# A gated two-layer block on one core: row statistics, the last head's sum and a few queue places are changed around the end of the long convolution and the start of attention

## The chip, the cores and the metric

The kernel runs on one core of a Trainium2 chip, which has eight. A core has five engines, each with its own in-order queue: TensorE (PE) for matrix products and transposes, VectorE (DVE), ScalarE (ACT), GpSimd (POOL), and SyncE (SP), which here only starts transfers. They work beside each other and wait for each other through semaphores. Sixteen DMA engines move data. The metric is the device time of one execution in microseconds (us), as a median of several. The profile is of one further execution.

## The reference, cut to what matters

The input `x` has 8 sequences of 256 rows of 512 numbers, 2048 rows in all, that is 16 tiles of 128 rows. Four parts add to it one after the other:

```python
x = x + tanh(g_xattn[0]) * L0_xattn(ctx, ctx, layernorm(x), ssm_kernel, D, 8)  # long convolution
x = x + tanh(g_ffn[0])   * L0_ffn(layernorm(x), w1, w2, w3)   # 512 -> 1408 -> 512
x = x + tanh(g_xattn[1]) * L1_xattn(layernorm(x), ctx, mask)  # attention over 256 keys
x = x + tanh(g_ffn[1])   * L1_ffn(layernorm(x), w1, w2, w3)   # 512 -> 2048 -> 512
```

The first part takes 32 heads of 8 channels. For each head it forms the products of all pairs of channels of `ctx`, convolves each pair along the 512 positions with the head's kernel (causal, with a skip term `D`), multiplies by the normalised `x` of the head, and sums over one of the two channel indices:

```python
kv  = einsum('bhil,bhjl->bijhl', k_, v_)      # k = v = ctx: symmetric in i, j
out = causal_conv(kv, ssm_kernel) + kv * D
out = einsum('bijhl,bhil->bjhl', out, q_)     # q = layernorm(x)
```

In the first feed-forward part each row is rounded to 8 bits by its own largest value, and the weights to -1, 0 or 1 by the mean of their absolute values:

```python
xq = clip(round(x * s), -128, 127) / s        # s = 127 / max|x| of the row
wq = clip(round(w * scale), -1, 1) / scale    # scale = 1 / mean|w|
h  = silu(xq @ w1q.T) * (xq @ w2q.T)
out = quantised(h) @ w3q.T
```

The second feed-forward part uses `sign(w)` times the mean absolute weight, and rounds its input in groups of 64.

## The kernel before, in words

The order of every engine's work is the order of the program text: the kernel asks for a manual schedule, so an instruction waits behind all that was written before it for the same engine.

**The convolution** runs over the heads, one head a step (`h`, steps 0 to 31). In the trace of before a step takes about 5 us: step 12 begins near 86, step 21 near 134, step 24 near 150, step 28 near 171 and step 31 near 187 us. In step h, in this order:

- `q_twice(h+1)` and `ctx_twice(h+3)`: two copies on ScalarE (both L290) into `qx` and `cx`. `pair_products(h+3)`: GpSimd forms `kv` (L303, L309) from `cx`.
- `half_products(h, 1)`: three DVE instructions (L348, L354, L361) multiply the second half of the head's convolution, which is in PSUM (`y`), by `qx` into `prod`. There are three `y` buffers, so these instructions free the buffer for a later convolution.
- the sum over the terms of `prod`. For most heads GpSimd adds its two halves (`add_halves`, L371), and a step later DVE sums the rest into `qT` (`reduce_terms`, L376). For the heads 12, 14, 19 and 21 (the set `alone`) DVE sums both halves itself (L378), in the same step, after the sum of the head before.
- `half_matmuls(h+1, 1)`: 14 of the products of PE, then 6 of `half_matmuls(h+2, 0)` later in the step (all L326). `half_wrap` (L336) is a small ScalarE copy in PSUM after each, and `half_products(h+1, 0)` comes between.
- jobs of a table, by slot: "load", "act", "dve", "pe", "act2", "pool", "late". Among them: loads of weights; the rounding of `L0_ffn` weights (`round_w0`, L447 on ScalarE, and `clip_w0`, L454 on GpSimd); transposes that bring finished rows back and add them to `x` (L395, L206); the statistics of finished rows (`ln_moments`, L116 and L117 on DVE); and, for the first rows of the feed-forward part, `front_norm` (L179), `front_max` (L483), `front_int` (L502, ScalarE, into `i8x`) and `front_turn` (L506 on GpSimd, then a transposing transfer that SP starts, L508).

Rows are taken in the order `order0`: the even tiles, then the odd ones. Heads 0 to 15 make the even tiles, heads 16 to 31 the odd tiles.

**The first feed-forward part** runs over the rows in 17 turns, `t` = 0 to 16 (`NT` is 16). A turn has three `up_block`s of 512, 512 and 384 columns of both weights (L792 on PE, L800 on ScalarE, L801 on DVE into `hh`). In turn t the row t-1 is rounded: its maximum (`row_max`, L483 on DVE), its integers (`i8h`, L942 on ScalarE), a clip on GpSimd (`qh`, L960) and a transposing transfer (`hqT`, L962). The `down0` products of row t-2 (L809) stand between the second and the third block. The front of row t+2 goes beside it, in turns 1 to 3 the odd tiles are brought back (`odd_back`: L395, L916, L917), and `ln_finish` turns four rows' moments into factors with three DVE instructions and fourteen short GpSimd instructions (L150 to L165). From turn 3 on two pieces of the last part's weights are loaded (`w1st`, L776) in each turn, and their signs are made on ScalarE (L780) at the end of the next turn.

**Attention** runs over the rows in the same way: scores (L878), `masked` (DVE), `exponentials` (L893), a transpose and its copy `eT` (L899, L901), the readout (L907), and again one or two sign pieces in each turn. `batch_gate` (L854, L856 on DVE) says whether a sequence has any valid key. In turn 16 of the part before, ahead of the last row's `i8h`, two sign pieces are made after the table load for Exp. The `down0` products of the rows 14 and 15 stand in turn 16 and in attention's turn 1. The last part is nearly all PE.

Of the kernel before, what the change touches and what calls it, by code (L numbers as in the profile page):

```python
# [21 lines left out]
P = 128  # L22
# [20 lines left out]
def flamingo_gated_kernel(  # L43
# [93 lines left out]
    def ln_moments_of(got, order, k, tag):  # L137

        g, j = k // GRP, k % GRP
        if g not in got:  # L140
            got[g] = small.tile([P, GRP, 2], F32, tag="mv" + tag, name="mv")
        ln_moments(got[g], j, order[k])

    def ln_finish(got, g, tag):
# [228 lines left out]
    def reduce_terms(h, added):  # L373
# [3 lines left out]
        else:  # L377
            nc.vector.tensor_reduce(  # L378
                o, prod.rearrange("p k a j d -> p (a j) k d"), AX.XY, ALU.add
            )  # L380

    trs = {}

# [67 lines left out]
    def clip_w0(i, k):  # L451
# [4 lines left out]
        )  # L456


    w1a = {}
# [40 lines left out]
    def front_int(k):  # L500
        i80[k] = pf1.tile([P, L], I8, tag="i8x", name="i8x")
        nc.scalar.activation(i80[k], xn0.pop(k), AF.Copy, scale=am0[k][1])  # L502
# [68 lines left out]
    for i, (a, b, c) in enumerate(STEPS0):  # L571
        for k in range(NL):
            job(a + k, "load", load_w0, i, k)
            job(b + k, "act", abs_w0, i, k)
            job(c[k], "act", round_w0, i, k)
            job(c[k] if i < 2 else (29, 30, 31, 31)[k], "pool", clip_w0, i, k)
        job(b + NL - 1, "dve", total_w0, i)
        job(b + NL, "act", spread, i)
        job(b + NL, "dve", mean_w0, i)
# [14 lines left out]
    for k in range(2):  # L594
# [3 lines left out]
        job(28 + k, "pool", front_turn, k)  # L598
    for k in range(GRP, 2 * GRP):
        job(24 + k, "dve", ln_moments_of, st0, order0, k, "0")  # L600

# [114 lines left out]
    for h in range(H):  # L716
        if h + 3 < H:
            load_toep(h + 3)
        if h + 4 < H:
            load_ch(h + 4)  # L720
        run(h, "load")
        if h + 1 < H:
            q_twice(h + 1)
        if h + 3 < H:
            ctx_twice(h + 3)
            pair_products(h + 3)
        half_products(h, 1)
        if h > 0 and h - 1 not in alone:
            reduce_terms(h - 1, True)
        if h in alone:  # L730
            reduce_terms(h, False)
        else:
            add_halves(h)
        if h + 1 < H:
            half_matmuls(h + 1, 1)
        run(h, "act")
        if h + 1 < H:
            half_wrap(h + 1, 1)
            half_products(h + 1, 0)
        run(h, "dve")  # L740
        if h + 2 < H:
            half_matmuls(h + 2, 0)
        run(h, "pe")
        run(h, "act2")
        if h + 2 < H:
            half_wrap(h + 2, 0)
        run(h, "pool")
        run(h, "late")
# [174 lines left out]
    for t in range(NT + 1):  # L923
# [7 lines left out]
        if t == NT:  # L931
            xn_[2] = normalised3(2)
            load_table(AF.Exp)
            for make in signs:
                make()
            signs = []
            ps_ = {k: scores(xT_.pop(k), keys[0]) for k in range(2)}
# [33 lines left out]
        if back:  # L971
            sums.append(odd_back(odds[back[-2]]))
        if t >= 2:
            hqT, f3 = hq_.pop(t - 2)
            d_[t - 2] = (down0(hqT), f3)
# [8 lines left out]
        if t < NT:  # L984
            up_block(*x0.pop(t), hh, 1024)
            h_[t] = hh
        if back:
            sums.append(odd_back(odds[back[-1]]))
# [3 lines left out]
        if t == 0:  # L992
            reduce_terms(H - 1, True)
        if t == 3:
# [4 lines left out]
        if t == NT - 3:  # L999
            p3 = pool(s_att, "p3", 2, reuse_waits="tile")  # L1000
            keys, values = {0: load_keys(0)}, {0: load_values(0)}
        for make in signs:
            make()
        signs = []
        if 3 <= t < NT:
# [4 lines left out]
        if t == NT - 1:  # L1010
            negs = {0: key_mask(bytes_.pop(0))}
            gates3 = {0: batch_gate(negs[0])}
        if t == NT:
# [394 lines left out]
```

## Time and profile before

| what | value |
|---|---|
| median of 3 runs | 740.42 us (739.88 to 740.97) |
| the profiled execution | 740.89 us |
| its span on the core | 739.1 us |
| PE busy | 711.0 us (96%) |
| DVE busy | 605.0 us (82%) |
| ScalarE busy | 363.7 us (49%) |
| GpSimd busy | 255.8 us (35%) |
| granted PE clock | 1.00 throughout |

A line of the timeline gives the start from the beginning of the span, the duration, the engine, the line of the kernel, the operation, what it writes and reads with shapes, and how many such instructions are merged. In brackets stand the idle time of the engine just before it, and what ended that. A line of waits gives the total, the number of times and the longest. A line of the stage table gives, after the stage's bounds and length, the busy time of PE, PE's weight loads, DVE, ScalarE and GpSimd with the number of instructions, then the granted clock, the share of the DMA engines and GB/s.

The whole span by stage: in the last part, from 327 us on, PE is busy 407.3 of 412.0 us. The convolution ends near 190 us, the first feed-forward part near 313 us and attention near 383 us.

### The profile page before, as it was taken

To read this page: it belongs to the slowest core of one execution; us is meant where nothing else is said; L and a number is where in the kernel's file an instruction comes from. 1 tells how busy PE (TensorE), PEld (TensorE's weight loads), DVE (VectorE), ACT (ScalarE), POOL (GpSimd) and SP (SyncE) were. 2 spreads that over 40 slices of the span, in tenths; PEclk is the share of its full clock that TensorE was granted. 3 is DMA by queue.
4 is the path that set the end of the run, shared out by engine and by line. 5 is a ranking of instruction groups with operands and counts; after the bars stand their busy time and mean duration, and the time that the engine had idled before them with its cause. 6 is when DMAs were issued, how large, how long until landed. Compare 5 with 4: busy or idle time off the path is not lost.

```text
span 739.1 us, 10041 instructions
## 1 busy us (share of the span) xinstructions
PE 711.0 (96%) x3172; PEld 528.3 (71%) x3172; DVE 605.0 (82%) x1232; ACT 363.7 (49%) x640; POOL 255.8 (35%) x360
## 2 busy tenths in 40 slices
PE   4999999999899999989999999999999999999997
PEld 3777777776454444556677788888888888888885
DVE  4799878898988889667777999888889888777965
ACT  5477877765577777758851223222223322222322
POOL 2898988888885444343310010000200002000000
PEclk9999999999999999999999999999999999999999
DMA  5675676831055557778613455445444545553443
GB/s 193 208 234 173 186 255 197 270 96 43 15 84 137 138 138 157 167 232 254 200 57 55 101 122 125 96 108 118 108 95 97 121 90 118 109 115 82 109 88 85
DMA packets 150444, 99.36 MB, mean 134 GB/s; under 512 B 84280, under 2 KB 128312, under 8 KB 150392
## 3 DMA queue, kind: packets, MB, share of 16 engines
q1 hardware_dynamic: 149608, 98.38, 51.3%
q0 software_dynamic: 256, 0.26, 0.5%
q8 instruction: 25, 0.41, 0.2%
q14 instruction: 27, 0.22, 0.1%
q10 hardware_dynamic: 528, 0.08, 0.1%
HBM read 75.58 MB, written 5.03 MB: 109 GB/s over the span
## 4 chain that ended last, share of the span: by engine, by line
PE 66%; DVE 4%; DMA 3%; issue 1%; POOL 1%; ACT 1%; SPq 0%; DVEq 0%; ACTq 0%; POOLq 0%
PE po L1283 16%; PE pb L1098 15%; PE pa L1098 15%; PE po L809 4%; PE po L907 4%; PE pb L792 4%; PE pa L792 4%; PE ps L878 3%; DMA hqT<-qh 1%; DMA w1st<-in_L_w2t 1%; DMA sT<-d 1%; PE tr L867 1%; DVE hh L801 1%; DVE st L116 0%; DVE qT L376 0%
## 5 line engine op out<-in xcount | busy, mean ns | idle before, releaser
L326 PE MATMUL y<-kv,toep 128*128 128x288 f32 x640 | 162.5, 411 | 4.4 <-DVE prod L361 4.2
L326 PEld LDWEIGHTS y<-kv,toep 128*128 128x128 f32 x640 | 120.3, 192 | 37.7 <-issue 2.0
L1106 ACT ACTIVATE sl<-pa,wmean 128x512 f32<-128x512 f32 x64 | 44.0, 688 | 187.2 <-PE pa L1098 187.2
L1098 PE MATMUL pa<-w,hi 128*128 128x512 f32 x256 | 100.7, 393 | 0.0
L1098 PE MATMUL pb<-w,hi 128*128 128x512 f32 x256 | 99.9, 390 | 0.6 <-DVE hh L1110 0.6
L1283 PE MATMUL po<-w,lo 128*128 128x512 f32 x256 | 100.0, 391 | 0.0
L1283 PE MATMUL po<-w,hi 128*128 128x512 f32 x256 | 99.8, 390 | 0.0
L1098 PE MATMUL pa<-w,lo 128*128 128x512 f32 x256 | 99.7, 390 | 0.0
L1098 PE MATMUL pb<-w,lo 128*128 128x512 f32 x256 | 99.7, 389 | 0.0
L159 POOL TENSOR_TENSOR nwt<-rstd 128x4 f32<-128x4 f32 x33 | 6.5, 198 | 240.5 <-DVE rstd L154 238.8
L303 POOL TENSOR_TENSOR kv<-cx 128x1024 f32<-128x1024 f32 x32 | 60.6, 1893 | 33.9 <-ACT cx L290 33.9
L371 POOL TENSOR_TENSOR prod<-prod 128x1024 f32<-128x1024 f32 x28 | 66.2, 2363 | 2.7 <-DVE prod L361 2.7
L792 PEld LDWEIGHTS <-xqT 128*128 128x128 bf16 x384 | 37.4, 98 | 41.4 <-issue 4.5
L1073 ACT CAST hi<-v 128x512 fp32r<-128x512 f32 x64 | 39.1, 621 | 48.6 <-DVE v L1273 48.6
L1110 DVE SCALAR_TENSOR_TENSOR hh<-pb,wmean,sl 128x512 f32<-128x512 f32 x64 | 47.7, 746 | 14.1 <-PE pb L1098 14.1
L1098 PEld LDWEIGHTS pb<-w,hi 128*128 128x128 f32 x256 | 48.1, 188 | 11.0 <-DVE hh L1110 1.0
L1283 PEld LDWEIGHTS po<-w,lo 128*128 128x128 f32 x256 | 48.1, 188 | 10.8 <-DVE lo L1078 1.0
L1098 PEld LDWEIGHTS pa<-w,hi 128*128 128x128 f32 x256 | 48.1, 188 | 10.3 <-issue 0.5
L1098 PEld LDWEIGHTS pa<-w,lo 128*128 128x128 f32 x256 | 48.1, 188 | 10.3 <-DVE lo L1078 0.2
L1283 PEld LDWEIGHTS po<-w,hi 128*128 128x128 f32 x256 | 48.1, 188 | 9.9
L1098 PEld LDWEIGHTS pb<-w,lo 128*128 128x128 f32 x256 | 48.1, 188 | 9.9
L348 DVE TENSOR_TENSOR prod<-y,qx 128x512 f32<-128x512 f32 x64 | 43.6, 681 | 10.9 <-ACT y L336 7.1
(142 smaller groups left out, 1325.3 us busy)
## 6 DMA issues: line engine op xcount, KB each, us to landing
sT<-d SPq DMA_DIRECT2D x64, 256.0 KB
toep<-ssm_skip SPq DMA_DIRECT2D x31, 256.0 KB
ch<-in_ctx_heads SPq DMA_DIRECT2D x32, 128.0 KB
w1a<-in_L_w1t SPq DMA_DIRECT2D x8, 512.0 KB
w1a<-in_L_w2t SPq DMA_DIRECT2D x8, 512.0 KB
w1st<-in_L_w1t SPq DMA_DIRECT2D x16, 256.0 KB
w1st<-in_L_w2t SPq DMA_DIRECT2D x16, 256.0 KB
cT<-in_ctx_t SPq DMA_DIRECT2D x8, 512.0 KB
```

The lines of the kernel that those rows point to most:

```text
L303: nc.gpsimd.tensor_tensor(kv[:, :, 0 : ND * HD].rearrange("p a (i d) -> p a i d", d=ND), cx[:, :, 0:HD].unsqueeze(3).to_broadcast([P, NL * ...
L326: nc.tensor.matmul(y[:, k, :, W0 : W0 + NPAIR], toeps[h][:, d * P : (d + 1) * P], kvs[h][:, mi * B : (mi + 1) * B, :].rearrange("p b n -> ...
L348: nc.vector.tensor_tensor(prod[:, 0, r, :, :], yv[:, :, W0 : W0 + ND * HD].rearrange("p a (i d) -> p a i d", d=ND), view(q, [HX, n], [1, H ...
L371: nc.gpsimd.tensor_tensor(flat[0], flat[0], flat[1], ALU.add)
L792: nc.tensor.matmul(pp[:, :fw], xqT[:, c, :], w0q[i][:, c, f0 : f0 + fw], start=(c == 0), stop=(c == NL - 1),)
L809: nc.tensor.matmul(po, hqT[:, c, :], w0q[2][:, c, :], start=(c == 0), stop=(c == NF0 - 1))
L907: nc.tensor.matmul(po, eT[:, c, :], cN[:, c, :], start=(c == 0), stop=(c == S // P - 1))
L1073: nc.scalar.copy(hi, v)
L1098: nc.tensor.matmul(pp, xT[k][:, c, :], w1q[i][:, c, f0 : f0 + 512], start=(c == 0 and k == 0), stop=(c == NL - 1 and k == 1),)
L1106: nc.scalar.activation(sl, pa, AF.Silu, scale=wmean1[:, 0:1])
L1110: nc.vector.scalar_tensor_tensor(hh, pb, wmean1[:, 1:2], sl, op0=ALU.mult, op1=ALU.mult)
L1283: nc.tensor.matmul(po, hT[b][k][:, c, :], w1q[2][:, b * NL + c, :], start=(b == 0 and c == 0 and k == 0), stop=(b == NB - 1 and c == NL - ...
```

## The change

1. `reduce_terms` of a head in `alone` moves from its own step to the next one, where the other heads have theirs.
2. The statistics of the rows 4 to 7 of `order0`, in before DVE's L116 and L117 in steps 28 to 31, are made on ScalarE by the new `moments_by_act`, at the ends ("late") of the steps 24, 25, 28 and 29.
3. The row 1's `i8x` gets a buffer of its own.
4. The last head's final sum, in before DVE's L376 at the end of turn 0, is made on GpSimd by the new `reduce_last` in step 31. The last weight piece's clip, in before GpSimd's L454 in step 31, is made on ScalarE by the new `clip_by_act`, with Sign, at the end of turn 0.
5. In turn 2 `down0` of row 0 moves behind the third `up_block`.
6. In turn 16 the two sign pieces are no longer made ahead of the last row's `i8h`; attention's turn 0 makes them after its `normalised3`. The first batch gate moves from the end of turn 15 into turn 16, behind the last row's maximum.

```diff
--- before.py
+++ after.py
@@ -141,6 +141,20 @@
             got[g] = small.tile([P, GRP, 2], F32, tag="mv" + tag, name="mv")
         ln_moments(got[g], j, order[k])
 
+    def moments_by_act(got, order, k, tag, junk):
+
+        g, j = k // GRP, k % GRP
+        if g not in got:
+            got[g] = small.tile([P, GRP, 2], F32, tag="mv" + tag, name="mv")
+        mean, var = got[g][:, j, 0:1], got[g][:, j, 1:2]
+        v = xs[:, order[k], :]
+        st = small.tile([P, nc.vector.BN_STATS_DIM], F32, tag="st", name="st")
+        nc.scalar.activation(junk, v, AF.Identity, accum_out=st[:, 0:1])
+        nc.scalar.activation(st[:, 1:2], st[:, 0:1], AF.Copy, scale=-1.0 / L)
+        nc.scalar.activation(junk, v, AF.Square, bias=st[:, 1:2], accum_out=st[:, 2:3])
+        nc.scalar.activation(mean, st[:, 0:1], AF.Copy, scale=1.0 / L)
+        nc.scalar.activation(var, st[:, 2:3], AF.Copy, scale=1.0 / L)
+
     def ln_finish(got, g, tag):
 
 
@@ -379,6 +393,12 @@
                 o, prod.rearrange("p k a j d -> p (a j) k d"), AX.XY, ALU.add
             )
 
+    def reduce_last(h):
+        prod, o = prods.pop(h), qT[:, :, h * HD : (h + 1) * HD]
+        half = prod[:, 1, :, :, 0:2]
+        nc.gpsimd.tensor_tensor(half, prod[:, 0, :, :, 0:2], prod[:, 0, :, :, 2:4], ALU.add)
+        nc.gpsimd.tensor_tensor(o, half[..., 0], half[..., 1], ALU.add)
+
     trs = {}
 
     def transpose_x(t, xn):
@@ -455,6 +475,12 @@
             q[:, a : a + n], w0r.pop((i, k))[:, :n], 1.0, -1.0, ALU.min, ALU.max
         )
 
+    def clip_by_act(i, k):
+
+        n, a = FW[i][k], sum(FW[i][:k])
+        q = w0q[i].rearrange("p c f -> p (c f)")
+        nc.scalar.activation(q[:, a : a + n], w0r.pop((i, k))[:, :n], AF.Sign)
+
 
     w1a = {}
     N1 = FF1 * L // P // 1024
@@ -498,7 +524,7 @@
         am0[k] = row_max(xn0[k], "x")
 
     def front_int(k):
-        i80[k] = pf1.tile([P, L], I8, tag="i8x", name="i8x")
+        i80[k] = (big if k == 1 else pf1).tile([P, L], I8, tag="i8x", name="i8x")
         nc.scalar.activation(i80[k], xn0.pop(k), AF.Copy, scale=am0[k][1])
 
     def front_turn(k):
@@ -573,7 +599,8 @@
             job(a + k, "load", load_w0, i, k)
             job(b + k, "act", abs_w0, i, k)
             job(c[k], "act", round_w0, i, k)
-            job(c[k] if i < 2 else (29, 30, 31, 31)[k], "pool", clip_w0, i, k)
+            if (i, k) != (2, 3):
+                job(c[k] if i < 2 else (29, 30, 31)[k], "pool", clip_w0, i, k)
         job(b + NL - 1, "dve", total_w0, i)
         job(b + NL, "act", spread, i)
         job(b + NL, "dve", mean_w0, i)
@@ -596,8 +623,12 @@
         job(26 + k, "dve", front_max, k)
         job(27 + k, "act", front_int, k)
         job(28 + k, "pool", front_turn, k)
-    for k in range(GRP, 2 * GRP):
-        job(24 + k, "dve", ln_moments_of, st0, order0, k, "0")
+    def first_by_act(k):
+        junk = p2.tile([P, L], F32, tag="xn", name="junk")
+        moments_by_act(st0, order0, k, "0", junk)
+
+    for k, h in enumerate((24, 25, 28, 29)):
+        job(h, "late", first_by_act, GRP + k)
 
 
 
@@ -725,11 +756,9 @@
             ctx_twice(h + 3)
             pair_products(h + 3)
         half_products(h, 1)
-        if h > 0 and h - 1 not in alone:
-            reduce_terms(h - 1, True)
-        if h in alone:
-            reduce_terms(h, False)
-        else:
+        if h > 0:
+            reduce_terms(h - 1, h - 1 not in alone)
+        if h not in alone:
             add_halves(h)
         if h + 1 < H:
             half_matmuls(h + 1, 1)
@@ -744,6 +773,8 @@
         run(h, "act2")
         if h + 2 < H:
             half_wrap(h + 2, 0)
+        if h == H - 1:
+            reduce_last(h)
         run(h, "pool")
         run(h, "late")
     assert not jobs
@@ -931,9 +962,7 @@
         if t == NT:
             xn_[2] = normalised3(2)
             load_table(AF.Exp)
-            for make in signs:
-                make()
-            signs = []
+            gates3 = {0: batch_gate(negs[0])}
             ps_ = {k: scores(xT_.pop(k), keys[0]) for k in range(2)}
         if t < NT:
             up_block(*x0[t], hh, 0)
@@ -970,7 +999,7 @@
         sums = []
         if back:
             sums.append(odd_back(odds[back[-2]]))
-        if t >= 2:
+        if t > 2:
             hqT, f3 = hq_.pop(t - 2)
             d_[t - 2] = (down0(hqT), f3)
         if t in FINISH:
@@ -984,13 +1013,17 @@
         if t < NT:
             up_block(*x0.pop(t), hh, 1024)
             h_[t] = hh
+        if t == 2:
+
+            hqT, f3 = hq_.pop(0)
+            d_[0] = (down0(hqT), f3)
         if back:
             sums.append(odd_back(odds[back[-1]]))
         for add in sums:
             add()
         sums = []
         if t == 0:
-            reduce_terms(H - 1, True)
+            clip_by_act(2, 3)
         if t == 3:
             s_conv.close()
             wp1 = pool(ctx, "w1", 1, reuse_waits="tile")
@@ -999,9 +1032,10 @@
         if t == NT - 3:
             p3 = pool(s_att, "p3", 2, reuse_waits="tile")
             keys, values = {0: load_keys(0)}, {0: load_values(0)}
-        for make in signs:
-            make()
-        signs = []
+        if t < NT:
+            for make in signs:
+                make()
+            signs = []
         if 3 <= t < NT:
             signs = [w1_signs(made + k) for k in range(2)]
             made += 2
@@ -1009,7 +1043,6 @@
             bytes_ = {b: load_mask(b) for b in range(2)}
         if t == NT - 1:
             negs = {0: key_mask(bytes_.pop(0))}
-            gates3 = {0: batch_gate(negs[0])}
         if t == NT:
             negs[1] = key_mask(bytes_.pop(1))
     s_mid.close()
```

## The prediction

> **What bounds the kernel now.** The page says TensorE (PE) is busy 711.0 us of the 739.1 us span, so a change can only win by closing PE's 28.1 us of idle time. I read first the busy table by stage, to place that idle time:
>
> ```profile
> core 0: us, PE busy (x) PEld busy (x) DVE busy (x) ACT busy (x) POOL busy (x), PEclk, DMA share, GB/s
> ...
> 85.00:150.00 65.00, 62.15 (x272) 48.55 (x271) 55.33 (x99) 48.63 (x88) 57.14 (x42) 1.00 0.72 235
> ...
> 171.00:190.00 19.00, 16.37 (x65) 11.10 (x65) 16.79 (x37) 10.55 (x19) 16.31 (x13) 1.00 0.13 28
> 190.00:212.00 22.00, 19.05 (x101) 9.90 (x100) 18.98 (x38) 14.09 (x21) 17.57 (x31) 1.00 0.29 42
> 212.00:305.00 93.00, 93.00 (x466) 45.77 (x465) 79.60 (x158) 72.11 (x102) 46.27 (x97) 1.00 0.61 145
> 305.00:327.00 22.00, 18.49 (x85) 11.32 (x83) 14.76 (x41) 13.37 (x26) 9.51 (x23) 1.00 0.68 179
> ```
>
> The stage's length less its PE time: 2.9, 2.6, 3.0, 0 and 3.5 us. With the start (10.9, until the first transpose) and the end (3.8, after the last product) these are nearly all of the 28.1. The first three lie at convolution steps 12 to 21, at its last steps and at the first feed-forward rows; the 3.5 is where attention begins. From 212 to 305 PE never waits: what is won before arrives whole at 305. Next, PE's waits:
>
> ```profile
> PE y L326 <- DVE prod L361: 4.2, 6, 1.5
> PE po L809 <- DMA hqT<-qh: 2.4, 3, 1.1
> PE pb L792 <- DVE hh L801: 1.7, 2, 1.3
> PE tre L899 <- ACT s L893: 1.1, 1, 1.1
> ```
>
> The convolution waits for VectorE (DVE), the later stages for one late transposed tile (hqT) and for ScalarE. Last, the timeline, for what is late in each:
>
> ```profile
> 137.38 2.28 DVE L378 TENSOR_REDUCE qT<-prod 128x256 f32<-128x2048 f32 x1
> ...
> 141.09 5.09 PE L326 MATMUL y<-kv,toep 128*128 128x288 f32 x20 [1.48 <-DVE prod L361]
> ```
>
> One long reduction (L378, 2.28) stands before the products that free PSUM for step 22: PE stands 1.48.
>
> ```profile
> 179.05 0.72 ACT L502 ACTIVATE i8x<-xn,sc 128x512 int8<-128x512 f32 x1 [3.95 <-POOL qx L506]
> ...
> 180.02 0.69 DVE L348 TENSOR_TENSOR prod<-y,qx 128x512 f32<-128x512 f32 x1 [1.60 <-ACT y L336]
> ...
> 188.87 1.02 PE L792 MATMUL pa<-w,xqT 128*128 128x512 bf16 x4 [1.06 <-DVE prod L361]
> ```
>
> ScalarE waits 3.95 for the single i8x buffer; its copy for step 29 is late, DVE idles 1.60.
>
> ```profile
> 198.03 1.60 DVE L483 TENSOR_REDUCE am<-hh 128x1 f32<-128x1408 f32 x1
> ...
> 201.60 1.36 POOL L960 TENSOR_SCALAR qh<-i8h 128x1408 bf16<-128x1408 int8 x1 [0.94 <-ACT i8h L942]
> ...
> 207.62 2.55 PE L809 MATMUL po<-w,hqT 128*128 128x512 bf16 x11 [0.99 <-DMA hqT<-qh]
> ```
>
> Row 0's maximum starts at 198.03, GpSimd's rounded row at 201.60, and PE waits for its transfer at 207.62.
>
> ```profile
> 311.42 1.27 ACT L780 ACTIVATE w<-w1st 128x512 fp32r<-128x512 f32 x2 [1.45 <-DMA w1st<-in_L_w2t]
> ...
> 312.59 1.45 ACT L942 ACTIVATE i8h<-hh,sc 128x1408 int8<-128x1408 f32 x1
> ...
> 314.13 1.36 POOL L960 TENSOR_SCALAR qh<-i8h 128x1408 bf16<-128x1408 int8 x1 [6.66 <-ACT i8h L942]
> ...
> 319.06 2.55 PE L809 MATMUL po<-w,hqT 128*128 128x512 bf16 x11 [1.14 <-DMA hqT<-qh]
> ```
>
> In attention's start two signs (L780), waiting for weights, stand before the last row's i8h, which GpSimd had awaited for 6.66 us.
>
> **Part by part.** The sum is made against the profiled execution's 740.89 us (span 739.1, 1.8 around it); the median shown is 0.47 lower. Clock times are "after (before)".
>
> *Both-halves reductions a step later.* The same four instructions. In step 21 DVE would do 1.35 (L376 to the next product) and 1.29 (products) from 136.24 and be done at 138.9 (140.9); PE is free at 139.61, so its wait goes, as do those at 92.58 (1.15) and 102.74 (0.23). PE gains 2.9, but from 136 to 178 DVE is idle only 0.28: it has the same work and leads only by what was won before, 1.15+0.23 = 1.4. That is the gain at step 22.
>
> *Statistics on ScalarE, steps 24 and 25.* A job is two passes of 512 elements with accumulation and three of one column. Rows: 0.63 and 0.19 for the read (L782), 0.28 for a column (L121): 2x0.82 + 3x0.2 (start to start) to 3x0.28 = 2.2 to 2.5; I take 2.2. It ends step h's ScalarE queue; behind it are the copies qx and cx of step h+1, for cx waits GpSimd (kv, 2.35), behind that its sum (2.36), and for that DVE's reduction. Step 24: PE, ahead by 1.9, lets the job run 155.3 to 157.5; cx ends 158.6 (158.2), kv 161.0, sum 163.4 (162.9). DVE wants it at 162.3 (163.34): 1.1 lost. Step 25's job (161.3 to 163.5) delays cx to 164.6 and the sum to 169.4; DVE loses 0.1. The products of step 28 then start at 173.75 (173.62): the 1.4 are gone. The Trainium skill, page "ScalarE: Activation LUTs", section "Rules for kernel authors", speaks against this edit: additions and multiplications belong on VectorE. DVE's pair L116/L117 costs 0.82, so by the rule four jobs lose 4x1.4 = 5.6 us of engine time. By the row for 171 to 190, ScalarE is busy 10.6 of 19.0 while DVE gates PE; I charge only the delays above. Bounds: 0 to 2.5 lost.
>
> *Steps 28 to 31.* A buffer for i8x of k=1 ends the 3.95 and the 1.60; DVE does no statistics (4x0.82). Against it: jobs 28 and 29 (2.2 each) stand before the copies qx of steps 30 and 31, so DVE stalls 0.45, 0.45 and 0.9. Walking the queues: products (29, second half) 177.65 (180.02), (30, second) 182.5 (184.76), (31, first) 186.05 (187.35), (31, second) 187.45 (189.46). PE's first up product, which needs the third of these done: 187.4 (188.87).
>
> *First rows.* DVE also loses the reduction L376 of head 31 (1.21), so row 0's maximum starts at 194.9 (198.03). GpSimd gets two sums of 512 and 256 elements and loses a clip (1.04). Nearest rows: L917 1.27 for 512, L309 0.46 for 128: together 1.9; bounds 1.2 and 3.0, as the operands are strided. On its queue behind them: a clip, row 2's front, fourteen short instructions (4.1). They end at 199.75, so the rounded row 0 starts there (201.60) though its input is ready at 198.4. With the same 4.6 of transfer, hqT lands at 205.8 (207.62). The clip on ScalarE (L420's 1024-element row: 1.06) falls in a gap; without that gap it would delay row 1 by 1.06. Row 2's transposes, issued at 195.4, hold PE until about 200, before hqT decides. The third block (1.31) no longer stands behind the down products: they run 205.8 to 208.2, and row 3 starts at 208.7 (211.75). **Gain 3.05**; bounds 1.5 (GpSimd 1.5 later) and 4.3 (PE without stalls).
>
> *Attention's start* (in the clock of before, without the 3.05). The batch gate (0.63 on DVE) goes behind row 15's maximum, so the scale is there at 309.5, and i8h starts when the table load ends: 309.97 (312.59). The rounding runs 311.45 to 312.8, hqT is issued at 312.9 (315.51), and the fourteen short instructions behind it end 2.7 earlier too, as does the key load (316.95) that SP issues behind hqT. The two signs do not vanish: they run 313.4 to 314.65, before the copy eT (315.0 against 315.15). So PE's readout starts at 315.0 (316.04) and ends at 316.8; hqT lands at 316.4 to 317.5, with a transfer of 3.55 (this one) to 4.6 (row 0's). Down products end 319.2 to 319.8 (321.44): 1.6 to 2.2. A further wait, 0.45 at 324.44 behind signs waiting for weights, may go. **Gain 2.0**, bounds 1.0 and 2.7. No transfer is added; w1st buffers come free 2 us later, but SP reaches their next load only at 315.1.
>
> *Sum.* 3.05 + 2.0 = 5.05; 740.89 - 5.05 = 735.8, and 0.47 off for the median: 735.4.
>
> **The rivals.**
> - *The job ends sooner or GpSimd catches up in step 26.* For: DVE's 0.28 wait there was short. Against: ScalarE started qx and cx as soon as it could. Then 1.2 more arrives: 734.1. Chance 0.2.
> - *Half is spent.* GpSimd's strided sums run long, or eT stays behind the signs and hqT lands late: 2 us less, 737.4. For: every gain passes GpSimd's queue or one transfer. Chance 0.2. Here also is a table load for Square. The skill's same page, "Table sets: the hidden batching unit", names copy, identity and abs as in every set; Square it does not. The trace shows four loads at L189, all asked for, and one at L1106 which nobody asked for, 1.28 each. By the page's 2.66 a switch, three switches (step 24, back for the square root of step 26, step 28) cost 8; by the row 3.8, giving 739.2. I take none: Abs, Copy and Identity ran beside Sqrt without one.
> - *Slower: the job's length.* Place: the end of steps 24, 25, 28, 29, before qx. Five instructions in a row each need the one before. If a job takes 4.0, all four delay DVE by 1.8 more, 7.2 in all: 742.5. It decides against the change above 2.2 + 5.05/4 = 3.5. Against: accumulator reads are followed within 0.09 by the next instruction. Chance 0.06.
> - *It moves waits only.* DVE stays the bound to 190, hqT lands as before: within 0.2% of 740.4. Chance 0.04.
>
> **How the numbers follow.** The first case has 0.5 with its own range 733.9 to 737.0. To leave out no more than 2 in 10 the range takes in the quicker case and most of the half-spent one: 733.2 to 738.4. This kernel's timing can tell 0.2%, 1.5 us. Faster than 738.9: 0.5+0.2+0.19 = 0.89; within: 0.05, table loads included; slower: 0.06.
>
> **What would show it.** Right: no PE wait at steps 12 to 21; no i8x wait near 175; DVE waiting for ScalarE copies or GpSimd sums in steps 26 to 31; the rounded row 0 near 200 and PE's wait moved behind the third block; i8h of the last row right behind the table load, hqT issued near 309.9 (312.9 less the 3.05 gained earlier), down products with a wait under 0.7. Wrong: a job over 3 us, a table load in step 24, or PE idle between rows 3 and 15, which would mean that the early gain was given back.

## The result and the profile after

The changed kernel takes 732.7 us (732.14 to 733.4, four runs) beside 740.15 (739.36 to 740.97) for the kernel before: ratio 0.990, 95% interval 0.988 to 0.992. Run a second time, among the experiments, it took 732.41 beside 740.84, ratio 0.989 (0.987 to 0.990). The forecast was 735.4 with a range from 733.2: the direction was right, the size too small by 2.7 us, and the range missed by 0.5.

The busy table by stage of the changed kernel, each stage placed where its work now lies (columns: busy time of each engine, clock, DMA share):

```profile
core 0: us, PE busy (x) PEld busy (x) DVE busy (x) ACT busy (x) POOL busy (x), PEclk, DMA share, GB/s
85.00:150.00 65.00, 64.88 (x285) 50.72 (x284) 56.88 (x102) 51.09 (x94) 58.20 (x41) 1.00 0.73 240
167.00:186.00 19.00, 16.89 (x69) 11.76 (x68) 16.85 (x36) 15.24 (x33) 18.15 (x14) 1.00 0.12 28
186.00:205.00 19.00, 18.02 (x98) 9.68 (x97) 15.80 (x28) 14.94 (x23) 16.38 (x29) 1.00 0.21 34
205.00:296.00 91.00, 91.00 (x456) 44.59 (x455) 79.25 (x158) 70.23 (x100) 47.15 (x98) 1.00 0.65 145
297.00:319.00 22.00, 19.67 (x90) 11.85 (x91) 15.64 (x42) 15.20 (x27) 9.39 (x22) 1.00 0.72 194
```

PE idles 0.1 us in the middle of the convolution (2.9 before), 2.1 at its end (2.6), 1.0 in the first rows (3.0) and 2.3 at attention's start (3.5). PE's waits, in us, times, longest:

```profile
PE po L938 <- ACT eT L932: 1.2, 1, 1.2
PE pa L823 <- DVE prod L375: 1.0, 1, 1.0
PE pb L823 <- DVE hh L832: 0.8, 2, 0.6
PE po L840 <- DMA hqT<-qh: 0.8, 1, 0.8
PE y L340 <- DVE rstd L126: 0.8, 1, 0.8
PE y L340 <- DVE prod L375: 0.2, 1, 0.2
```

The convolution's wait for VectorE's products is down from 4.2 to 0.2; a further 0.8, put down to VectorE's `rstd`, was 0.2 before. The wait for hqT is no longer that of row 0: it is a new one in row 13. The wait for eT has grown from 0.4 to 1.2.

**How traces are compared here.** Before the first changed instruction is reached, one trace can already be ahead of another: the third copy `cx` of the convolution starts at 23.44 in the kernel before and 22.25 in the changed one, and in the 18 traces of this study it lies between 22.07 and 23.44, with identical code up to there. So 1.19 of the 7.8 us between the two spans is chance. The table takes it off: every figure is the start of an event less its start in the kernel before, less the same difference at the third `cx`. Negative is earlier. The column "head 23" is VectorE's first product of head 23 (142.79 in the kernel before). The last column gives the median, and in brackets the median less that of the kernel before on the same chip.

| kernel | start of 3rd cx | head 23 | first up product | row 0 rounded (qh) | row 4 rounded | first scores | 4th eT | end of span | median us |
|---|---|---|---|---|---|---|---|---|---|
| changed | 22.25 | -0.73 | -2.82 | -3.62 | -5.34 | -4.21 | -6.16 | -6.61 | 732.7 (-7.45) |
| a1_after_again | 23.25 | -0.76 | -2.84 | -3.59 | -5.51 | -4.47 | -7.48 | -7.91 | 732.41 (-8.43) |
| u1_sums_own_step | 23.14 | -0.03 | -0.19 | -0.99 | -2.70 | -1.03 | -2.77 | -3.10 | 735.99 (-3.68) |
| u2_stats_dve | 22.07 | -1.80 | -4.03 | -4.03 | -5.76 | -4.95 | -6.59 | -7.03 | 733.36 (-6.31) |
| u3_one_i8x | 22.61 | -1.26 | -2.18 | -2.49 | -4.81 | -3.58 | -6.71 | -6.97 | 733.67 (-6.00) |
| u4_last_sum_dve | 23.05 | -1.39 | -3.47 | -4.74 | -5.84 | -5.84 | -7.48 | -8.01 | 731.11 (-8.56) |
| u5_down_before | 22.16 | -0.81 | -2.90 | -3.69 | -4.44 | -3.20 | -6.34 | -6.72 | 733.71 (-6.45) |
| u6_signs_first | 22.90 | -1.22 | -3.29 | -4.09 | -5.80 | -4.72 | -5.32 | -5.86 | 734.93 (-5.23) |
| j2_job_twice | 23.07 | -1.32 | -0.61 | -1.29 | -2.92 | -1.98 | -5.11 | -5.23 | 735.36 (-4.80) |
| j0_no_passes | 22.75 | -0.99 | -3.19 | -4.00 | -5.66 | -5.43 | -7.85 | -8.11 | 732.3 (-8.25) |
| j4_late_no_passes | 23.06 | -0.96 | -4.14 | -4.13 | -5.85 | -4.79 | -7.53 | -7.92 | 731.45 (-9.39) |
| d1_sum_dve | 22.38 | -0.96 | -3.06 | -4.83 | -5.92 | -5.93 | -7.91 | -8.34 | 731.85 (-8.70) |
| m1_mask_later | 23.13 | -1.26 | -3.37 | -4.18 | -5.90 | -5.12 | -8.22 | -8.59 | 733.12 (-7.43) |
| m2_mask_sp | 22.63 | -1.10 | -3.20 | -3.98 | -5.90 | -5.83 | -8.64 | -8.89 | 731.92 (-8.92) |
| b1_dve_both | 23.35 | -1.35 | -3.59 | -3.56 | -4.65 | -4.66 | -7.35 | -7.21 | 733.26 (-7.29) |
| b7_d1_signs | 22.67 | -0.78 | -2.89 | -4.67 | -5.72 | -5.72 | -8.80 | -9.13 | 730.82 (-10.02) |
| control | 23.13 | -0.27 | -0.26 | -0.23 | -0.42 | -0.43 | -0.18 | -0.29 | 740.29 (+0.13) |

The start is not the only chance. In step 20 ScalarE's copy `cx` of head 23 waits for the load of its `ch`, in the changed kernel 1.87, but 0.85 in u2_stats_dve, where the code is the same up to there. In the changed kernel:

```profile
128.49 0.62 ACT L304 COPY cx<-ch 128x512 f32<-128x512 f32 x1 [1.87 <-DMA ch<-in_ctx_heads]
```

and in u2_stats_dve

```profile
127.27 0.62 ACT L304 COPY cx<-ch 128x512 f32<-128x512 f32 x1 [0.85 <-DMA ch<-in_ctx_heads]
```

In the fifteen traces of kernels with part 1 this wait lies between 0.85 and 1.88, and VectorE's lead at head 23 is 2.6 less this wait in each of them. So what differs between those fifteen in the column "head 23" is chance too, for all other edits come later. The first up product less this column is -2.07 to -2.11 in the six traces that have the same code up to there (changed, a1, u5, u6, m1, m2), where without it they differ by 0.55. Below, "from head 23 on" means that this column is taken off. Row 4 from head 23 on is then -4.58 to -4.80 in five traces that have the same code up to it (changed, a1, u6, m1, m2), so less than 0.25 there is not read from one trace. Later comes more: at the fourth eT the two traces of the changed kernel itself differ by 1.3.

### The profile page after: what moved, and what is told of

Same layout as the page of the kernel before. It is cut to its first block, busy times and chain, and to the rows that moved or that the text cites. A ratio compares the mean times of both kernels' runs of the same rounds, so it can differ in the third digit from the quotient of the medians.

```text
span 731.3 us, 10063 instructions
## 1 busy us (share of the span) xinstructions
PE 709.6 (97%) x3172; PEld 527.1 (72%) x3172; DVE 602.8 (82%) x1223; ACT 371.5 (51%) x669; POOL 256.3 (35%) x361
## 4 chain that ended last, share of the span: by engine, by line
PE 84%; DVE 4%; POOL 4%; ACT 2%; DMA 2%; issue 2%; SPq 0%; DVEq 0%; ACTq 0%; POOLq 0%
PE po L1316 16%; PE pb L1131 16%; PE pa L1131 16%; PE y L340 15%; PE po L938 4%; PE po L840 4%; PE pa L823 4%; PE pb L823 4%; PE ps L909 3%; POOL prod L385 2%; DVE am L509 1%; POOL kv L317 1%; DMA hqT<-qh 1%; DMA w1st<-in_L_w2t 1%; DVE hh L832 1%
```

## Experiments

All edits are against the changed kernel. Medians are of four to six runs (14 for the control). Each group of kernels ran on one chip together with the kernel before, whose median there lay between 739.67 and 740.84. So a kernel is also compared by its gain over the kernel before on its chip; the changed kernel's gains are 7.45 and 8.43.

**Its parts undone, one at a time.** The sums of the heads 12, 14, 19 and 21 back in their own step:

```
-        if h > 0:
-            reduce_terms(h - 1, h - 1 not in alone)
-        if h not in alone:
+        if h > 0 and h - 1 not in alone:
+            reduce_terms(h - 1, True)
+        if h in alone:
+            reduce_terms(h, False)
+        else:
             add_halves(h)
```

> The changed kernel, but heads 12, 14, 19 and 21 are summed in their own step again (part 1 undone). My theory: part 1 is what puts PE 2.9 us ahead, and that lead covers the ScalarE jobs of steps 24 and 25; without it PE waits 1.2 and 1.5 us at steps 12 and 21 again, and in step 26 DVE waits about 1 us for a GpSimd sum. Loses 2.0 to 2.9 us against the changed kernel: about 735. Rival (the parts add up independently): only what the prediction gave the part, 1.4 us, about 734.1, and no DVE wait in step 26.

735.99 us, ratio 0.995 (0.994 to 0.997): 3.3 to 4.8 lost in medians and gains. In the trace the part is worth 2.6 at row 4 (5.34 less 2.70), as the first theory said; the 1.4 of the rival falls. PE's waits of 1.13 (at 92.26) and 1.45 (at 140.75) are back. Two waits of VectorE in this kernel show why it is more than the 1.4 of lead:

```profile
159.29 0.69 DVE L362 TENSOR_TENSOR prod<-y,qx 128x512 f32<-128x512 f32 x1 [0.59 <-ACT qx L304]
...
164.52 1.22 DVE L390 TENSOR_REDUCE qT<-prod 128x256 f32<-128x1024 f32 x1 [0.99 <-POOL prod L385]
```

Without PE's lead the statistics jobs of steps 24 and 25 hold up the copy qx and GpSimd's sum, and VectorE waits 0.59 and 0.99. In the changed kernel neither wait exists. From head 23 to the products of step 28 this kernel loses 1.5, where the changed one gains 0.4. Why the times lose more than the trace stays open.

The statistics of rows 4 to 7 back on VectorE:

```
-    for k, h in enumerate((24, 25, 28, 29)):
-        job(h, "late", first_by_act, GRP + k)
+    for k in range(GRP, 2 * GRP):
+        job(24 + k, "dve", ln_moments_of, st0, order0, k, "0")
```

> The changed kernel, but the four rows' statistics are on DVE in steps 28 to 31 again (part 2 undone). My theory: 4 x 0.82 us come back to DVE, which bounds these steps, less the DVE stalls that the jobs cause there (0.4, 0.3 and 1.1 in the changed kernel): loses 1.5 to 2.5 us, about 734.7. Rival (the rule that this work belongs on VectorE, the jobs cost as much as they save): within 0.5 us of 732.7 or faster.

733.36 us, ratio 0.992 (0.990 to 0.993). At the first up product, from head 23 on, this kernel is 0.14 ahead of the changed one (-2.23 against -2.09): up to there the move to ScalarE wins nothing, and the rival, which spoke with the rule of the Trainium skill that the forecast quotes (page "ScalarE: Activation LUTs", section "Rules for kernel authors": additions and multiplications belong on VectorE), is right. Then VectorE still has the last of the four pairs, 0.82, ahead of row 0's maximum. Row 0 is rounded 0.6 to 0.7 later than in the changed kernel and row 4 is 0.7 to 0.8 later; the median is 0.7 to 1.0 longer and the gain 1.1 to 2.1 smaller. So the move is worth about half of what the theory said by the trace, and 0.7 to 2.1 by the times; the rival's "within 0.5" is missed narrowly.

One buffer for i8x again:

```
-        i80[k] = (big if k == 1 else pf1).tile([P, L], I8, tag="i8x", name="i8x")
+        i80[k] = pf1.tile([P, L], I8, tag="i8x", name="i8x")
```

> The changed kernel with one i8x buffer again (part 3 undone). My theory: ScalarE waits some 4 us for GpSimd in step 28, the copy and the job behind it are late, DVE idles 1.6 us or more: loses 1.5 to 2.5 us, about 734.7. Rival (DVE has other work to fill the wait since it has no statistics to do): under 0.5 us.

733.67 us, ratio 0.991 (0.990 to 0.993). From head 23 on the first up product comes 1.2 later, row 0's rounding 1.6 and row 4 1.1 to 1.2 later; the median is 1.0 to 1.3 longer, the gain 1.4 to 2.4 smaller. So the wait is paid, at the lower end of the 1.5 to 2.5 or somewhat under it.

The last head's sum back on VectorE, the last clip back on GpSimd:

```
-        if h == H - 1:
-            reduce_last(h)
...
-            clip_by_act(2, 3)
+            reduce_terms(H - 1, True)
```

> The changed kernel with the last head's sum on DVE and the last clip on GpSimd again (part 4 undone). My theory: row 0's maximum starts 1.2 us later, GpSimd's queue is 0.65 us shorter; PE's waits in row 1 grow by about 1: loses 0.5 to 1.2 us, about 733.6. Rival (GpSimd's queue sets the first rows): gains up to 0.6 us.

731.11 us, ratio 0.988 (0.987 to 0.990): 1.3 to 1.6 under the changed kernel's medians, and 0.1 to 1.1 more gained. The expected loss did not come. GpSimd's timeline in this kernel:

```profile
196.47 1.36 POOL L986 TENSOR_SCALAR qh<-i8h 128x1408 bf16<-128x1408 int8 x1 [0.45 <-ACT i8h L968]
...
295.22 1.31 POOL L869 DMA_DIRECT2D mu<-in_mask  x2 [3.66 <-PE pa L820]
```

GpSimd now waits 0.45 for row 0's i8h, where in the changed kernel the row waits for GpSimd, and row 0 is rounded 0.5 earlier from head 23 on. At row 4 the kernel is no earlier than the changed one (-4.45 against -4.61 and -4.75); the 0.7 to 1.0 that it is ahead at the first scores is won in row 13. The second line shows how, further down.

Row 0's down products ahead of row 2's third block again:

```
-        if t > 2:
+        if t >= 2:
             hqT, f3 = hq_.pop(t - 2)
```

(and the block `if t == 2:` behind the third up block left out).

> The changed kernel with row 0's down products before the third block again (part 5 undone). My theory: the transposed row lands about 4.2 us after its issue at 198.2, near 202.4, and PE would be there at 201.0: it waits 1.3 us, about 734.0. Rival (the transfer is early enough by now): no change.

733.71 us, ratio 0.992 (0.990 to 0.993). The wait for hqT is back (0.87 at 201.91), and 1.0 to 1.1 is lost at row 4 from head 23 on; somewhat less than expected.

The signs ahead of the last row's i8h again, and the batch gate ahead of the last maximum:

```
         if t == NT:
-            gates3 = {0: batch_gate(negs[0])}
+            for make in signs:
+                make()
+            signs = []
...
```

> The changed kernel with the two sign pieces ahead of the last row's integers and the batch gate ahead of its maximum again (part 6 undone). My theory: loses the 1.9 us that the traces show between rows 14 and attention's turn 2, about 734.6. Rival (that part of the trace was won by other means): under 0.5 us.

734.93 us, ratio 0.993 (0.991 to 0.995): 2.2 to 3.2 lost, about as expected. From the first scores to the fourth eT this kernel wins 0.6, the changed one 1.95 and on its second run 3.0.

**The statistics job.** The jobs of steps 24 and 25 done twice:

```
+        if k < GRP + 2:
+            moments_by_act(st0, order0, k, "0", junk)
         moments_by_act(st0, order0, k, "0", junk)
```

> The changed kernel, with the jobs at the ends of steps 24 and 25 done twice over (1.94 us more of ScalarE work each, same results). The step of the prediction that failed said that these jobs delay a GpSimd sum and with it DVE. My theory: the chain copy, products, sum is there, and the changed kernel just escapes it (DVE's reduction starts within 0.05 us of the sum's end); twice the job then costs nearly its length: 2 to 3.5 us, about 735.5, with DVE waiting for a GpSimd sum in steps 26 and 27. Rival (the jobs lie in idle time of ScalarE with room to spare): under 0.5 us.

735.36 us, ratio 0.994 (0.992 to 0.995): 1.94 more in each of two jobs costs 2.7 to 3.6 in medians and gains and 3.0 to 3.2 at row 4 from head 23 on. VectorE waits 1.00 and 0.25 for GpSimd's sums, and 1.10 and 0.66 for the copies qx behind the jobs. Past its present length a job is on the path.

The same jobs cut to two one-column instructions, their moments left out:

> The changed kernel, whose statistics jobs of steps 24 and 25 are cut to two one-column instructions: the moments of those two groups are left out (a copied and an absolute column stand in their place), so each job shrinks from the measured 1.94 us to about 0.4; the jobs of steps 28 and 29 stay. With both jobs doubled, 2.2 to 2.7 us were lost. Theory (job covered up to its present length: GpSimd's sum ends at 160.95 just as VectorE wants it at 160.98, so only what exceeds 1.94 costs): taking them out gains at most 0.6, median 732.1 to 732.9 and PE's first up product (less the start) within 0.7 of the changed kernel's -2.82. Rival (the charge of 1.2 at steps 24 and 25 that the prediction made is paid, only other terms were too small): 1.2 to 1.6 gained, median 731.1 to 731.5, first up product at -4.0 to -4.4. Second rival (each us of ScalarE there costs in proportion, as doubling suggests): 2.0 to 2.4 gained, median about 730.5.

732.3 us, ratio 0.989 (0.987 to 0.991), row 4 from head 23 on at -4.67, as in the changed kernel (-4.61 and -4.75): nothing won, although the copy `cx` of step 25 comes 1.7 earlier. From head 23 to the products of step 28 this kernel gains 0.5, like u2 and b1, which have no such job; the changed kernel and all others with part 1 and a job of that length gain 0.4. Up to its present length the job costs 0.1. This is the experiment that decides on the forecast's charge of 1.2.

The jobs of steps 28 and 29 cut in the same way:

> The changed kernel, whose statistics jobs of steps 28 and 29 are cut to two one-column instructions (the moments of those two groups are left out); the jobs of steps 24 and 25 stay. The prediction charged these two jobs with stalls of VectorE of 0.45, 0.45 and 0.9 at steps 30 and 31. If that is paid: first up product 1.0 to 1.8 earlier than the changed kernel (-4.2 to -5.0 less the start), median 731.0 to 731.8. Rival (as at steps 24 and 25 a job of 1.94 is covered): within 0.4 of the changed kernel, first up product -2.8 to -3.6, median 732.2 to 733.1.

731.45 us (729.96 to 732.56), ratio 0.987 (0.984 to 0.989). PE's first up product comes 1.1 earlier from head 23 on, so these two jobs do stall VectorE, as the forecast charged; 0.1 to 0.3 of it is left at row 4, no more than chance. The median is 1.0 under that of the changed kernel on the same chip, inside the spread of these runs.

**The last sum and the mask loads.** The sum back on VectorE, the clip kept on ScalarE:

```
-        if h == H - 1:
-            reduce_last(h)
...
+            reduce_terms(H - 1, True)
             clip_by_act(2, 3)
```

> The changed kernel with the last head's reduction on VectorE again (at the end of row turn 0, as before), but the last clip of w0 still as a sign on ScalarE. Undoing both won 1.4 us (731.1 against 732.7). Theory (the GpSimd sums, 1.69 us, are the loss, as they stand before fourteen short instructions and the rounded row 0): the rounded row 0 starts with its input, about 0.45 earlier than with both undone, since GpSimd has one clip fewer: 195.6 to 196.5 less the start; median 730.6 to 731.6. Rival (taking the clip off GpSimd is what mattered and the sign on ScalarE is in the way of row 1's scaling): as the changed kernel, 732.4 to 733.0.

731.85 us (730.35 to 732.48), ratio 0.988 (0.986 to 0.989). The trace agrees with the theory (row 0's rounding 1.0 earlier than in the changed kernel from head 23 on), the median is 0.25 above the band given. At row 4 it is 0.2 to 0.35 ahead of the changed kernel, at the first scores 1.3 to 1.5, so most of it is won in row 13. The sum on GpSimd is what costs; the clip's move does not, as against u4 the clip on ScalarE wins 0.5 at row 4.

Sum and statistics both back on VectorE (the edits of u2 and u4 together):

> A candidate for a better version: the changed kernel with part 2 (statistics) and part 4 (last sum, clip) both undone, so only the sums a step later, the second i8x buffer, the third block ahead of row 0's down products and the signs behind the last row remain. If the two add, 1.4 from part 4 and 0 from part 2: 730.9 to 731.5. If VectorE, which then has both the moments and the last reduction in steps 28 to 31, becomes the bound there (4 x 0.82 and 1.21 more): 732.2 to 733.5.

733.26 us, ratio 0.990 (0.989 to 0.992): VectorE is the bound, as the second case said. Against u4, which differs only by the statistics, 2.1 are lost in the median (1.3 in the gain) and 1.15 at row 4 from head 23 on; PE waits 1.30 at 197.12 for VectorE's hh. With the sum on GpSimd the statistics' move was worth 0.7 to 0.8 there (u2). So the two moves are in part substitutes, and the statistics are the better one to move.

The changed kernel loses 1.1 between row 4 and the first scores. Its timeline in row 13:

```profile
291.29 2.25 SPq L991 DMA_TRANSPOSE hqT<-qh  x1
291.60 1.31 POOL L872 DMA_DIRECT2D mu<-in_mask  x2
...
297.50 2.55 PE L840 MATMUL po<-w,hqT 128*128 128x512 bf16 x11 [0.83 <-DMA hqT<-qh]
```

GpSimd's loads of two mask rows are issued 0.3 behind the transposing transfer, which lands 6.2 after its issue. In the kernel before, control, u4, d1, b1 and b7, where the last sum is on VectorE, these loads wait 2.5 to 3.7 for PE (u4's second line above) and row 13 has no wait, though row 14 has one of 0.2 to 0.6. In the others that have them on GpSimd's queue the loads start 0.3 behind the transfer. The loads written one row turn later:

> The changed kernel with the loads of both mask rows issued in row turn 15 instead of at the end of turn 14, so that they do not land beside row 13's transposing transfer. Theory (row 13's hqT lands 6.2 us after its issue because the mask loads run beside it, and PE waits 0.83 for it and loses 1.1 in rows 13 to 15): hqT of row 13 in under 5 us, no wait at row 13's down products, gain from row 4 kept until the last row (ps0 at -5.3 rather than -4.2); median 731.4 to 732.1. Rival (row 13's tile was late for another reason, or row 14's or 15's now pays, or the masks come too late for the first scores): no change within 0.4, median 732.3 to 733.1, the wait moved to row 14 or 15.

733.12 us, ratio 0.990 (0.988 to 0.991). The edit did not do what it was for: GpSimd, with nothing ahead of it, issued the loads at 291.87, and PE waited 0.53. It leaves the question open. The loads on SyncE's queue instead:

```
-        nc.gpsimd.dma_start(out=mu, in_=mask[b].partition_broadcast(P))
+        eng = nc.sync if b < 2 else nc.gpsimd
+        eng.dma_start(out=mu, in_=mask[b].partition_broadcast(P))
```

> The changed kernel with the loads of the first two mask rows issued by SyncE, behind row 13's transposing transfer on one queue, not by GpSimd beside it (moving the GpSimd load one turn later had not moved it in time: 291.87 against 291.60). In all kernels with the last sum on VectorE this load waits 2.5 to 3.7 us for TensorE and rows 13 to 15 lose nothing; in those with the sum on GpSimd it does not wait and 0.8 to 1.1 us are lost. Theory (the two transfers share the DMA engines): hqT of row 13 lands in 4.4 to 5 us, wait at its down products under 0.2, ps0 at -5.3 to -5.9 less the start; median 731.4 to 732.2. Rival (SyncE's own issue of the mask delays row 14's transfer or the w1st loads by as much, or row 13 was late for another reason): ps0 at -4.0 to -4.8, median 732.3 to 733.3.

731.92 us, ratio 0.988 (0.986 to 0.990):

```profile
291.06 2.27 SPq L992 DMA_TRANSPOSE hqT<-qh  x1
294.49 0.90 SPq L873 DMA_DIRECT2D mu<-in_mask  x2
296.28 2.54 PE L840 MATMUL po<-w,hqT 128*128 128x512 bf16 x11
...
303.93 2.55 PE L840 MATMUL po<-w,hqT 128*128 128x512 bf16 x11 [0.37 <-DMA hqT<-qh]
```

Row 13's products start with no wait, at most 5.2 after the issue, and the first scores are 1.0 to 1.3 ahead of the changed kernel's from head 23 on: as the theory has it, though row 14 now waits 0.37. The Trainium skill, page "Trainium Kernel Development and Optimization", section "Key Constraints", says that transfers issued by SyncE, ScalarE and GpSimd share the same DMA engines and interleave; the 6.2 against 5.2 fits that. It is not the whole account. Of the eleven traces in which the loads start 0.3 behind row 13's transfer, ten have a wait of 0.5 to 1.4 there, but j0 waits only 0.05; of the seven in which they do not, none waits. What let j0's transfer land sooner is not known. Why the loads wait for PE only where the sum is on VectorE was not found out.

**Level, and a better version.** The changed kernel once more:

> The changed kernel itself once more, since the predicted range was missed by 0.5 us and single runs of one kernel spread over 1.4 us at the third convolution step already. If the miss is in the mechanism (1.2 charged at steps 24 and 25 and not paid): median 732.2 to 733.2 again, and the stages less the start as in the first trace (step 25 -0.8 to -1.4, first up product -2.8 to -3.5, row 4 -5.3 to -5.9, last row 4.2 to 5.2). Rival (the first four runs were lucky, the change is inside the range): 733.3 to 734.2.

732.41 us (732.09 to 733.04), ratio 0.989 (0.987 to 0.990). The level stands, and the miss is not a matter of four lucky runs. The kernel before, run as a kernel of its own:

> The kernel before, unchanged, for a second trace of it. In the two traces that I have, 1.2 us of the difference arise before 24 us, ahead of the first changed instruction, while PE's first products run slowly. If that is chance from run to run, this trace's first convolution products will turn fast at another time than in the first one; time 740.2. If it comes with the kernel, it repeats the first trace to 0.1 us.

740.29 us, ratio 1.001 (1.000 to 1.002); its stages lie within 0.43 of those of its first trace.

The sum back on VectorE, and one sign in place of two in attention's first turn:

```
-    SIGNS = [2, 2, 2, 2, 1, 2, 1, 1, 2, 1, 2, 1, 1, 1, 1]
+    SIGNS = [1, 2, 2, 2, 2, 2, 1, 1, 2, 1, 2, 1, 1, 1, 1]
```

> A candidate: the changed kernel with the last sum back on VectorE (the clip stays on ScalarE), and with one sign in place of two in the first attention turn (the other comes in the sixth), so that the second copy eT does not stand behind a sign that waits for weights. With the sum alone 731.85, and PE's readout still waited 0.7 us for eT. Theory: that wait goes, 0.5 to 1.0 gained, median 730.6 to 731.5. Rival (the readout then waits for hqT or the last row's tile instead, or the sixth turn pays): as before, 731.5 to 732.4.

730.82 us (730.27 to 731.32), ratio 0.986 (0.985 to 0.988). None of its runs reaches those of the changed kernel on the same chip (732.09 and more): this version beats both kernels. Its gain is 10.0, the changed kernel's there 8.4. Its second eT waits for PE and no longer for signs:

```profile
314.45 0.37 ACT L930 COPY eT<-tre 128x256 f32<-128x256 f32 x1 [0.72 <-PE tre L928]
```

## Why the forecast was too small

**Both-halves sums.** Right in kind: the waits at steps 12 to 21 are gone. The 1.4 at step 22 was about right as a lead of VectorE: at head 23 it is 2.6 less the wait for `ch`, so 1.2 with the 1.45 that the kernel before waits, and 0.73 in the changed kernel's trace, where the load came later. But PE's own lead, which the working put at 2.9 and then did not count, pays for what follows.

**Statistics, steps 24 and 25: the step that failed.** The forecast said "PE, ahead by 1.9, lets the job run 155.3 to 157.5", and from that 1.2 lost. The timeline after, in its own clock (add 1.19 for that of before):

```profile
152.95 0.30 ACT L350 COPY y<-y 128x192 f32<-128x192 f32 x1 [0.80 <-ACT y L350]
153.17 0.64 ACT L152 ACTIVATE junk<-xs 128x512 f32<-128x512 f32 x1
...
155.11 0.60 ACT L304 COPY qx<-qT 128x512 f32<-128x512 f32 x1
...
158.58 2.37 POOL L385 TENSOR_TENSOR prod<-prod 128x1024 f32<-128x1024 f32 x1
160.98 1.22 DVE L390 TENSOR_REDUCE qT<-prod 128x256 f32<-128x1024 f32 x1
...
171.29 0.67 DVE L362 TENSOR_TENSOR prod<-y,qx 128x512 f32<-128x512 f32 x1
```

The job runs from 154.36 to 156.30 in the clock of before: 0.94 earlier than forecast, as PE was 2.7 ahead and not 1.9, and 0.26 shorter (1.94 for five instructions, not 2.2). GpSimd's sum ends at 160.95, and VectorE, with no gap, starts on it at 160.98. The products of step 28 start at 171.29, so 172.48, where the forecast had 173.75: 1.27 better, about the charge. j0 shows that only 0.1 of it is paid, j2 that it is paid beyond this length, and u1 that it is paid once PE's lead is gone: there the 1.5 is lost that the forecast had between its lead of 1.4 and 173.75. The rival "the job ends sooner or GpSimd catches up", 734.1, had this mechanism. That number lies inside the forecast's range; the rest of the miss comes from the first rows. Square brought no table load: the trace has five, in the same places as before.

**Steps 28 to 31.** Right:

```profile
172.10 0.71 ACT L528 ACTIVATE i8x<-xn,sc 128x512 int8<-128x512 f32 x1
...
178.07 0.69 DVE L362 TENSOR_TENSOR prod<-y,qx 128x512 f32<-128x512 f32 x1 [0.39 <-ACT qx L304]
...
179.76 0.69 DVE L362 TENSOR_TENSOR prod<-y,qx 128x512 f32<-128x512 f32 x1 [0.31 <-ACT y L350]
...
183.35 0.69 DVE L362 TENSOR_TENSOR prod<-y,qx 128x512 f32<-128x512 f32 x1 [1.08 <-ACT qx L304]
```

i8x no longer waits, and VectorE's three stalls are 0.39, 0.31 and 1.08, where 0.45, 0.45 and 0.9 were forecast. The first up product (184.86, so 186.05) is 1.35 better than the 187.4 forecast, the same error carried along. That the statistics' move as a whole wins nothing up to here, and shows only from row 0's rounding on (u2), was not said.

**First rows.** The chain was right, two terms in it were too long:

```profile
192.57 1.62 DVE L509 TENSOR_REDUCE am<-hh 128x1 f32<-128x1408 f32 x1
...
196.79 1.36 POOL L989 TENSOR_SCALAR qh<-i8h 128x1408 bf16<-128x1408 int8 x1
...
198.18 2.40 SPq L991 DMA_TRANSPOSE hqT<-qh  x1
...
202.40 2.54 PE L840 MATMUL po<-w,hqT 128*128 128x512 bf16 x11
...
205.21 1.03 PE L823 MATMUL pa<-w,xqT 128*128 128x512 bf16 x4
```

GpSimd's queue holds up row 0, as forecast: its input is ready at 196.1 and it starts at 196.79. The two sums took 1.69 (1.9 forecast), and the transfer had landed 4.06 after its issue at the latest, when PE loads its first weights from it (4.6). So PE starts the down products right behind the third block, with no wait, and row 3 at 205.21, so 206.4 (208.7 forecast). Of these 2.3, 1.35 come from steps 24 and 25, 0.54 from the transfer and 0.4 from GpSimd's queue. The forecast priced the GpSimd sums but saw no loss in them against VectorE; by d1 and u4 the move costs 0.7 to 1.5 by the first scores, most of it in row 13, and 0.1 to 1.6 in medians and gains.

**Rows 4 to 15.** "From 212 to 305 PE never waits: what is won before arrives whole" failed: 1.1 is given back at row 13, most likely to mask loads that the change set free (m2 for it, j0 against a plain rule). The forecast had named PE idle between rows 3 and 15 as a sign of being wrong, but had no cause for it; the loss hid part of the error the other way.

**Attention's start.** 2.0 forecast, 1.95 measured:

```profile
304.48 1.45 ACT L971 ACTIVATE i8h<-hh,sc 128x1408 int8<-128x1408 f32 x1
306.01 1.36 POOL L989 TENSOR_SCALAR qh<-i8h 128x1408 bf16<-128x1408 int8 x1 [4.66 <-ACT i8h L971]
...
311.00 2.55 PE L840 MATMUL po<-w,hqT 128*128 128x512 bf16 x11
...
316.16 0.63 ACT L811 ACTIVATE w<-w1st 128x512 fp32r<-128x512 f32 x1 [1.43 <-DMA w1st<-in_L_w2t]
...
317.10 1.98 PE L938 MATMUL po<-cN,eT 128*128 128x512 f32 x4 [1.17 <-ACT eT L932]
```

i8h stands right behind the table load and the row's down products need no wait. The further 0.45 of wait behind signs that "may go" became 1.17 in this trace and 0.2 in the second, with the landing of w1st (in the control the 0.45 is not there either); in b7 it does not occur.

**The sum.** 5.05 forecast; with 2.3 more at row 3, 1.1 less in row 13 and 0.4 more behind the fourth eT it is the 6.6 of the table. The remaining 1.2 between the two traces is the chance at the start. The two medians differ by 7.45 and 8.4 in the two sets of runs, against 7.9 less the start in the second trace, where attention's start won 3.0.

## What to carry to other kernels

A delay put on an engine's queue is only paid once it outruns the lead of the engine that feeds it: follow that lead, not just that of the bound engine; a kernel with the job cut and one with it doubled show both sides. When one engine is relieved, the first move may bring most of it; a second one to a slower queue (here the last sum on GpSimd, ahead of fourteen short instructions) can take back what the first has won. A load that has waited was scheduled by that wait: ask of every wait that a change takes away which transfer the load will now run beside. And before two traces are compared, look for what differs ahead of the first edit: here one load's landing moved all that came behind it by up to 1.0.

## What was not expected of the hardware

A tiny VectorE instruction took 1.40 beside a GpSimd clip. It occurs eleven times in the trace and takes 0.17 the other ten times; this first one takes 0.17 in six of the 18 traces, 1.35 to 1.40 in eight, and between in four:

```profile
190.32 1.47 POOL L474 TENSOR_SCALAR w<-w0r 128x1536 bf16<-128x1536 int8 x1
190.41 1.40 DVE L166 TENSOR_SCALAR nwi<-nwv 128x4 int32<-128x4 int32 x1
```

Both end together. The Trainium skill, page "SBUF — State Buffer", section "SBUF: two separate sides", speaks of a port pair that VectorE, in some of its instructions, shares with GpSimd, and that one instruction holds until it ends; the two lines fit that, but no run here tested it. And the first 23 us of one and the same code differed by up to 1.4 us between traces, and the wait for one load (`ch` of head 23) by 1.0.
